# The last image's softmax done one row of sub-images at a time, in another order of sub-images, with spills and one x load issued later

## The chip, the cores and the metric

The kernel runs on one core of a Trainium2 chip. The metric is device time in microseconds (us) of one execution, and lower is better. TensorE is called PE, VectorE DVE, ScalarE ACT, GpSimd POOL and SyncE SP. Line numbers such as L1211 are those of the kernel before, unless the text says that they are those of the changed one.

## The reference

Two layers follow each other on x, of 4 images, 256 channels and 64 by 64 pixels, all in 32 bits.

```python
# layer 0: 49 logits per pixel, then attention over a dilated 7x7 window
k = conv(x, w1, padding=6, rhs_dilation=2) + b1       # 256 -> 128, 7x7
k = conv(k, w2) + b2                                  # 128 -> 49, 1x1
attn = softmax(k, axis=1)
xp = pad(x, 6)
shifts = stack([xp[:, :, 2*u:2*u+64, 2*v:2*v+64] for u in range(7) for v in range(7)], axis=1)
x = einsum('bkchw,bkhw->bchw', shifts, attn)
# layer 1: iterative whitening in 4 groups of 64 channels
Sigma = EPS * I + cov(x - mean);  rTr = 1 / trace(Sigma)
P = I;  5 times: P = 1.5 P - 0.5 P^3 (Sigma rTr)
out = (P sqrt(rTr)) (x - mean) * weight + bias
```

## The kernel before

**Convolution.** The two convolutions of layer 0 are one 7 by 7 convolution from 256 channels to 49 logits. It is done by evaluation at points: DVE (L347 to L354) and ACT (L541, L547) evaluate x at the points (`xh`), PE multiplies each bank of points by its weights `wr` (L599, into the two PSUM tiles `cv`), ACT and DVE take the banks out (`pv`, L610), and DVE interpolates (`zz`, `lgx`). ACT adds the bias at L731, after which an image's logits are complete. Each image has rows of banks, three banks to a row.

**Sub-images.** Since the window is dilated by 2, an image splits into four sub-images of 32 by 32 pixels by the parity of row and column. Sub-image n = 4b, ..., 4b + 3 of image b is (h, pc): h is the parity of the row and picks one of two x slots of the image, pc is the parity of the column. The order is (0, 0), (0, 1), (1, 0), (1, 1).

**Softmax.** `softmax(b, pc)` turns the logits of one column parity, both rows h, to pixels on partitions (PE, L991), and does maximum, Exp, sum and scaling. For images 0 to 2 ACT does the Exp in 16 pieces with the bias taken in; for the last image DVE subtracts the maximum (L1006) and ACT does Exp over each row at once (L1013). Four DVE shuffles (L1035) follow over both rows together; the result is `d`.

**Terms and bands.** `move_terms(n)` copies the terms of one sub-image into `zt` in eleven copies, on ACT for images 0 to 2 (L1076) and on DVE for the last (L1088). Eight POOL DMAs write them to DRAM (`sd`, L1093; two buffers that alternate over n). `load_band(n, half)` reads them back with SP DMAs as the banded matrices `band` (L1128) and `bandz` (L1139). There is one buffer for each half.

**Weighted sum.** `make_block` turns a block of x by PE (L1169) and evicts it into `xb` (L1175) and, for the middle blocks, `xbz` (L1183); `xb` has four buffers, and the turned tiles `tp` in PSUM have three. These evictions are ACT's for images 0 to 2 until the convolution is over, and from then on (`tail`) DVE's. `weighted_sum` multiplies blocks by bands (L1211) into `y`. `store_y` puts y back into the x slot (ACT L1231; in the tail its second half on DVE, L1229). `turn_y` turns it (PE L1242) and ACT copies it into `yt` (L1250), and `moments` accumulates the covariance `sig` (PE L1263).

**Halves.** Each sub-image is done by `first_half(n)` and `second_half(n)`, written here as f0, s0, f1, s1 and so on. A first half also turns the last four tiles of the sub-image before and adds their moments; `finish()` does the same where no first half follows. In a first half the order on PE is: turn 4 and 5 of the sub-image before, matmuls of block (0,0), block (1,0), turn 6, matmuls of (0,1), block (1,1), turn 7, block (2,0), matmuls of (1,0), block (2,1), matmuls of (1,1), matmuls with `bandz`, store, moments, blocks (3,0) and (3,1). A second half ends by turning the first two blocks of the next sub-image.

**Order.** PE runs its instructions in the order in which the program is written. On the other engines a scheduler orders them by priority, and each engine's queue is then run in that order. The convolution of image b is cut into eight stretches, and `gap(b, j)` after each runs what `plan` put there: the softmax of image b - 1 in gaps 0 and 1, and halves of the sub-images before. For image 2 its halves are planned from gap 4 of image 3 on, so f8 is in gap 4, s9 in gap 7, and f10 follows the convolution. After the convolution comes the tail: f10, the softmax for pc 0 of the last image, s10, the softmax for pc 1, f11, s11, f12 and so on to s15, all in the order of `todo`. Then layer 1's iterations run (some 664 to 677 us), and the result is made and stored (677 to 728 us).

**x slots.** Images use slots of x in SBUF. After an image's row is stored, `move(k)` for k = 0, 1, 2 spills the slot's y to DRAM (POOL, L1281, 2 MB in one DMA) and loads the x of slot 5, 6 or 7 into its place from a DRAM copy, `ahead` (POOL, L161). `load_x` loads x from the input in four POOL DMAs (L147). The spilled slots come back in the tail. POOL issues its DMAs in the order of its queue, and the profile shows 0.53 us for each `sd` write and 1.69 us for each `load_x` piece.

Of the kernel before, what the change touches and what calls it, by code (L numbers as in the profile page):

```python
# [32 lines left out]
def kernel(  # L33
# [29 lines left out]
    nc = tc.nc  # L63
# [875 lines left out]
        "p (q r c w) -> p q r c w", q=Q8, r=2, c=NCC  # L939
    )  # L940
    row_eval(0, 5, [rb[0], rb[1], xrs[5]])
    for s in range(2):
        load_x(s, s, nc.gpsimd)
    col_interp(0, 1)
    col_interp(0, 2)
    direct0(4, 1)
# [30 lines left out]
        yt_buf.append(a)  # L977


    def softmax(b, pc):  # L980

        lv = logits[b].rearrange("p r w -> p (r w)")
        nm = f"{b}_{pc}"
        mx = work.tile([P, NCH, 2], F32, tag="mx", name=f"mx_{nm}")
        lt = []
        for hf in range(2):
            t = cv_buf[hf] if b == B - 1 else tp()
            lt.append(t.rearrange("p (i h k) -> p i h k", i=NI, h=2))
            for i in range(NI):
                pe(  # L990
                    nc.tensor.transpose(  # L991
                        lt[hf][:, i].rearrange("p h k -> p (h k)")[:, :K2],
                        lv[:K2, bass.ds(2 * (NI * hf + i) * P + pc, P, 2)],
                        ident[:K2, :K2],
                    )
                )
            nc.vector.tensor_reduce(
                mx[:, NI * hf : NI * (hf + 1)], lt[hf][:, :, :, :KT], AX.X, ALU.max
            )
        nc.vector.tensor_scalar(mx, mx, -1.0, None, ALU.mult)  # L1000
        d = terms[b, pc] = bpool.tile([P, 2, NCH, KT], F32, tag="d", name=f"d_{nm}", bufs=2)
        s = work.tile([P, 2, NCH], F32, tag="s", name=f"s_{nm}")
        if b == B - 1:
            for hf in range(2):
                half = slice(NI * hf, NI * (hf + 1))
                nc.vector.tensor_tensor(  # L1006
                    d.rearrange("p h i k -> p i h k")[:, half],
                    lt[hf][:, :, :, :KT],
                    mx[:, half].unsqueeze(3).to_broadcast([P, NI, 2, KT]),
                    ALU.add,  # L1010
                )
            for h in range(2):
                nc.scalar.activation(d[:, h], d[:, h], AF.Exp)  # L1013
                nc.vector.tensor_reduce(s[:, h], d[:, h], AX.X, ALU.add)
        for h in range(2):
            for i in range(NCH) if b < B - 1 else ():
                nc.scalar.activation(  # L1017
                    d[:, h, i], lt[i // NI][:, i % NI, h, :KT], AF.Exp,
                    bias=mx[:, i, h : h + 1], accum_out=s[:, h, i : i + 1],
                )  # L1020
            nc.vector.reciprocal(s[:, h], s[:, h])
            rm = work.tile([P, NCH, KS], F32, tag="rm", name=f"rm_{nm}_{h}")
            nc.vector.tensor_tensor(
                rm,
                s[:, h].unsqueeze(2).to_broadcast([P, NCH, KS]),
                cmask.unsqueeze(1).to_broadcast([P, NCH, KS]),
                ALU.mult,
            )
            dh = d[:, h].rearrange("p i (u v) -> p i u v", u=KS)
            nc.vector.tensor_tensor(  # L1030
                dh, dh, rm.unsqueeze(2).to_broadcast([P, NCH, KS, KS]), ALU.mult
            )
        dv = d.rearrange("p h i (u v) -> p (h i u) v", u=KS)
        for step, vs in ((1, slice(4, 7, 2)), (2, slice(5, 7)), (-1, slice(0, 3, 2)), (-2, slice(0, 2))):
            last = nc.vector.stream_shuffle(  # L1035
                dv[:, :, vs], dv[:, :, vs], [(c - step) % SW for c in range(SW)]
            )

        return last

    terms, moved, loaded = {}, set(), set()

    MOVES = [(0, 0, 4), (2, 0, 2), (2, 2, 2)]
    MOVES += [(s, j, 1) for s in (1, 3) for j in range(CR)]

    def move_terms(n, after=None):

        b, h, pc = n // 4, n // 2 % 2, n % 2
        if n in moved or n >= 4 * B or (b, pc) not in soft_done:
            return  # L1050
        moved.add(n)
        zt = zts[n % 2]
# [3 lines left out]
        for k, (s, j0, nj) in enumerate(MOVES):  # L1056
            u = (s + R) % CR
            m, g = divmod(j0 + u - R, CR)
            ne = 2 if u + CR < KS else 1
            i = d[j0 * SW : (j0 + nj) * SW, :, u : u + CR * (ne - 1) + 1 : CR]  # L1060
            i = bass.AP(
                tensor=i.tensor,
                offset=i[:, :, :, KS - 1].offset,
                ap=[*(list(a) for a in i.ap[:-1]), [-1, KS]],
            )
            o = zt[g * SW : (g + nj) * SW]
            e = R + KS * m + KS - 1 - u
            o = bass.AP(
                tensor=o.tensor,
                offset=o[:, e].offset,  # L1070
                ap=[list(o.ap[0]), [KS * WS, NCH], [(KS - CR) * WS, ne], [1, KS]],
            )

            with tc.high_priority() if n == 0 else nullcontext():
                if b < B - 1:
                    ins = nc.scalar.copy(o, i)  # L1076
                    if after is not None:

                        tc.add_manual_dep(
                            ins.ins,  # L1080
                            after.ins.name,
                            mybir.DependencyInfo(
                                mybir.DependencyClass.NoSync, mybir.DependencyReason.DATA
                            ),
                            reason="move_terms",
                        )
                else:
                    nc.vector.tensor_copy(o, i)  # L1088
        D = sd[n % 2][:]
        for g in range(CR):  # L1090
            for h in range(2):
                p0 = g * SW + h * TC
                nc.gpsimd.dma_start(  # L1093
                    bass.AP(
                        tensor=D.tensor,
                        offset=D.offset + h * HS + g * RS,
# [3 lines left out]
                        "p (m e) w -> p m (e w)", e=KS  # L1100
                    ),
                )

    back = []

# [11 lines left out]
    def load_band(n, half):  # L1117
# [28 lines left out]
            )  # L1146
        if (n, half) == (4 * B - 1, 1):
            bring_back(dma)

    blocks = {}  # L1150

    tail = []

    def tile_of(t, cc, t8, h, pc):

# [1 line left out]

    def where(n):

        return slots[n // 2], n % 2  # L1160

    def make_block(n, m):

# [3 lines left out]
        for cc in range(NCC):  # L1167
# [2 lines left out]
                    t[:, cc * P : (cc + 1) * P], tile_of(xt, cc, t8, h, pc), ident  # L1170
                )
            )
        xb = bpool.tile([P, C], F32, tag="xb", name=f"xb_{n}_{t8}{h}", bufs=4)
        with tc.high_priority():
            (nc.vector.tensor_copy if tail else nc.scalar.copy)(xb, t[:, :C])  # L1175
        blocks[n, m] = xb
        if t8 in (1, 2):
            z = ("z", 2 - t8)
# [1 line left out]
                blocks[n, z] = bpool.tile([P, C], F32, tag=f"xbz{t8}", name=f"xbz_{n}_{t8}")  # L1180
            i = slice(0, 64) if t8 == 2 else slice(64, P)
            with tc.high_priority():
                (nc.vector.tensor_copy if tail else nc.scalar.copy)(  # L1183
                    blocks[n, z][h * 64 : (h + 1) * 64], t[i, :C]
                )

# [89 lines left out]
    def move(k):  # L1276

        nxt_k = {0: 5, 1: 6, 2: 7}.get(k)
        if nxt_k is not None:
            spill[k] = dram.tile([P, NCC * SH * W], F32, name=f"spill{k}")  # L1280
            nc.gpsimd.dma_start(spill[k], slots[k].rearrange("p a r w -> p (a r w)"))  # L1281
            load_x(k, nxt_k, nc.gpsimd)

    open_n, done, soft_done = [], {-1}, set()

    half_done = {-1}

# [6 lines left out]
        if n % 2:  # L1294
            move(n // 2)

    def first_half(n):
        last = open_n.pop() if open_n else None

        def turn(i):  # L1300
            if last is not None:
                turn_y(last, i)

        for m in PIECES[0][:2]:
            if (n, m) not in blocks:
                make_block(n, m)
        turn(4)
        turn(5)
        weighted_sum(n, 0, 0)
        make_block(n, PIECES[0][2])  # L1310
        turn(6)
        weighted_sum(n, 0, 1)
        make_block(n, PIECES[0][3])
        turn(7)
        make_block(n, PIECES[1][1])
        weighted_sum(n, 0, 2)
        make_block(n, PIECES[1][2])
        weighted_sum(n, 0, 3)
        weighted_sum(n, 0, 4)
        move_terms(n + 1, store_y(n, 0))  # L1320
        half_done.add(n)
        load_band(n + 1, 0)
        if last is not None:
            moments(last, 1)
            if last % 2:
                move(last // 2)
        make_block(n, PIECES[1][3])
        make_block(n, PIECES[1][4])

    def bands(n, after=None):  # L1330

# [4 lines left out]
            load_band(n, 1)  # L1336
            move_terms(n + 1, after)

    def second_half(n):
        turn_y(n, 0)  # L1340
        turned = turn_y(n, 1)
        if n % 4 == 3:
# [5 lines left out]
        turn_y(n, 3)  # L1348
        weighted_sum(n, 1, 3)
        weighted_sum(n, 1, 4)  # L1350
        last = store_y(n, 1)
        moments(n, 0)
        open_n.append(n)
# [5 lines left out]


    NPC = 8
    todo = {}

    def plan(b, j, *what):
        todo.setdefault((b + j // NPC, j % NPC), []).extend(what)

    def soft(b, pc):
        with tc.high_priority() if pc == 0 else nullcontext():
            last = softmax(b, pc)
        soft_done.add((b, pc))  # L1370
        if pc == 0 and (b == 0 or tail):
            bands(4 * b)

    for b in range(B):
        hs = [
            (lambda n=n, f=f: f(n))
            for n in range(4 * b, 4 * b + 4)
            for f in (first_half, second_half)
        ]
# [5 lines left out]
                    plan(b + 1, 2 + j, finish)  # L1385
        else:
            for j in range(8):
                plan(b + 1, 4 + j, hs[j])
    for b in range(B):
        for j in range(2) if b else ():  # L1390
            plan(b + 1, j, lambda b=b, j=j: soft(b, j))
    plan(1, 2, lambda: load_x(4, 4, nc.gpsimd))
# [39 lines left out]
        slots[k] = rpool.tile([P, NCC, SH, W], F32, name=f"back{k}")  # L1432
        back.append(k)
    tail.append(True)
    for k in sorted(todo):
        gap(*k)
    finish()


# [215 lines left out]
```

## Time and profile before

| | |
|---|---|
| median of three runs | 741.35 us (739.52 to 743.1) |
| the profiled execution | 735.81 us, of which the span is 734.0 us |
| PE / DVE / ACT / POOL busy | 684.0 / 598.0 / 328.8 / 133.2 us |
| mean granted clock of PE | 0.977 |
| last convolution matmuls (L599) end | 554.1 us |
| logits of the last image complete (L731) | 565.2 us |
| first halves f10, f11, f12, f13 | 9.65, 20.08, 9.04, 7.88 us |
| second halves s9 to s13 | 6.0 to 6.3 us |

The span runs from the first to the last instruction of the profiled execution. Shares of busy time are over that span. The granted clock is a share of PE's full speed. In a line of the timeline the first number is the start and the second the duration of a group of instructions, and the brackets name the idle time of that engine just before and what ended it.

### The profile page before, as it was taken

Reading aid. Unit: us, or ns where it says so; the run is one execution under the profiler, and the core shown is the slowest. Engines: PE = TensorE matmul, PEld = TensorE weight load, DVE = VectorE, ACT = ScalarE, POOL = GpSimd, SP = SyncE. Lnnn points to the kernel's source line nnn. Section 1 sums busy time; section 2 is a strip of 40 time slices with the busy share of each in tenths; the row PEclk is TensorE's granted clock in tenths of the full one; section 3 lists DMA queues with packets and bytes.
Section 4 is the critical chain, followed back from the end, with each engine's and each line's share of the span. In section 5 each row is a group of like instructions: output and inputs, shape, how many; then the busy total and the mean of one; then the engine's idle time right before and its main releaser. Section 6 shows DMA issues by size and latency. Waiting matters only on the chain.

```text
span 734.0 us, 19103 instructions
## 1 busy us (share of the span) xinstructions
PE 684.0 (93%) x7728; PEld 539.1 (73%) x7728; DVE 598.0 (81%) x1291; ACT 328.8 (45%) x919; POOL 133.2 (18%) x194
## 2 busy tenths in 40 slices
PE   6999999999898999998999999998999689997996
PEld 1449543478898988897999989888998678885231
DVE  3799998995796899999886899899998885435575
ACT  1424320133654655675545445716546222332564
POOL 0002526663021020020220200200211322100000
PEclk9999999999999999999999999999999979997899
DMA  8923999973665582157645820452641535472687
GB/s 322 259 92 103 239 387 212 229 179 90 169 173 150 206 299 68 60 188 257 173 111 201 266 69 1 104 168 72 166 103 37 106 75 126 107 271 117 246 354 316
DMA packets 78337, 126.10 MB, mean 172 GB/s; under 512 B 36471, under 2 KB 58664, under 8 KB 77096
## 3 DMA queue, kind: packets, MB, share of 16 engines
q1 hardware_dynamic: 59912, 64.52, 26.9%
q0 software_dynamic: 12288, 42.08, 21.8%
q10 hardware_dynamic: 6048, 18.27, 8.0%
q8 instruction: 61, 1.00, 0.5%
q14 instruction: 28, 0.23, 0.1%
HBM read 78.78 MB, written 52.36 MB: 179 GB/s over the span
## 4 chain that ended last, share of the span: by engine, by line
PE 38%; DVE 27%; issue 9%; ACT 6%; DMA 4%; POOL 4%; ACTq 0%; SPq 0%; POOLq 0%; DVEq 0%
PE cv L599 15%; PE y L1211 7%; PE tp L1595 4%; DVE xh L354 3%; PE tp L1242 3%; DMA band<-sd 3%; DVE pv L354 3%; POOL ahead L147 3%; PE sig L1263 3%; DVE zz L354 2%; PE tp L1169 2%; DVE rb L347 2%; DVE rb L354 2%; ACT d L1017 1%; DVE pv L350 1%
## 5 line engine op out<-in xcount | busy, mean ns | idle before, releaser
L599 PE MATMUL cv<-xh,wr 128*49 128x128 f32 x4160 | 231.5, 273 | 3.5 <-ACT xh L547 3.3
L599 PEld LDWEIGHTS cv<-xh,wr 128*49 128x49 f32 x4160 | 226.3, 124 | 6.9 <-ACT xh L547 3.5
L1211 PE MATMUL y<-band,xb 128*128 128x209 f32 x512 | 113.4, 348 | 7.0 <-DMA band<-sd 5.9
L1093 POOL DMA_DIRECT2D sd<-zt x128 | 67.3, 532 | 234.1 <-ACT zt L1076 159.9
L1211 PEld LDWEIGHTS y<-band,xb 128*128 128x128 f32 x512 | 87.8, 195 | 8.9 <-DMA band<-sd 4.8
L610 ACT COPY pv<-cv 113x486 f32<-113x486 f32 (+2 forms) x60 | 26.1, 435 | 95.6 <-PE cv L599 90.5
L1250 ACT COPY yt<-tp 128x256 f32<-128x256 f32 x128 | 45.4, 378 | 50.3 <-PE tp L1242 49.2
L1242 PE MATMUL tp<-ident,slot 128*128 128x128 f32 x256 | 51.4, 298 | 9.0 <-ACT yt L1250 6.7
L354 DVE SCALAR_TENSOR_TENSOR pv<-pv 113x162 f32<-113x162 f32 x176 | 53.1, 322 | 3.3 <-ACT pv L610 2.6
L1242 PEld LDWEIGHTS tp<-ident,slot 128*128 128x128 f32 x256 | 41.1, 205 | 15.9 <-ACT yt L1250 7.8
L1169 PE MATMUL tp<-ident,slot 128*128 128x128 f32 x256 | 50.0, 300 | 2.7 <-DVE xbz L1183 1.4
L1231 ACT ACTIVATE slot<-y,pivot 128x512 f32<-128x512 f32 x52 | 36.1, 741 | 34.5 <-PE y L1211 34.4
L1169 PEld LDWEIGHTS tp<-ident,slot 128*128 128x128 f32 x256 | 40.9, 204 | 6.2 <-DVE xbz L1183 1.8
L147 POOL DMA_DIRECT2D slot<-in_x_dram x20 | 33.9, 1695 | 50.6 <-issue 46.2
L1076 ACT COPY zt<-d 32x112 f32<-32x112 f32 (+2 forms) x132 | 38.2, 290 | 7.3 <-DVE d L1035 5.4
L1263 PE MATMUL sig<-yt 128*64 128x65 f32 x1024 | 37.7, 228 | 0.0
L1263 PEld LDWEIGHTS sig<-yt 128*64 128x64 f32 x1024 | 33.2, 140 | 5.7 <-issue 4.3
L354 DVE SCALAR_TENSOR_TENSOR xh<-ct 128x512 f32<-128x512 f32 x40 | 26.7, 689 | 12.4 <-PE cv L599 12.3
L1017 ACT ACTIVATE d<-tp,mx 128x49 f32<-128x49 f32 x96 | 27.5, 337 | 19.8 <-DVE mx L1000 19.8
L764 PE MATMUL acc<-slot,tap 128*49 128x256 f32 (+7 forms) x224 | 34.8, 468 | 0.0
L1175 ACT COPY xb<-tp 128x256 f32<-128x256 f32 x82 | 28.5, 376 | 11.6 <-PE tp L1169 11.1
L1229 DVE TENSOR_SCALAR slot<-y,pivot 128x512 f32<-128x512 f32 x12 | 9.0, 751 | 27.2 <-ACT slot L1231 27.1
(239 smaller groups left out, 1117.3 us busy)
## 6 DMA issues: line engine op xcount, KB each, us to landing
out_dram<-out SPq DMA_DIRECT2D x32, 512.0 KB, 3.6
band<-sd SPq DMA_DIRECT2D x64, 242.0 KB, 3.3
slot<-in_x_dram POOLq DMA_DIRECT2D x20, 512.0 KB, 7.1
sd<-zt POOLq DMA_DIRECT2D x128, 77.0 KB, 3.1
wr<-gd ACTq DMA_DIRECT2D x14, 588.0 KB, 5.3
wr<-gd ACTq DMA_DIRECT2D x14, 490.0 KB, 4.3
ahead<-in_x_dram POOLq DMA_DIRECT2D x12, 512.0 KB, 7.3
spill<-slot POOLq DMA_DIRECT2D x3, 2048.0 KB, 7.2
```

Of the source, the lines that this page charges most:

```text
L147: queue.dma_start(o[:, cc, h], src[:, :, pr, h * SW : (h + 1) * SW])
L354: return in_turn(STT(o, a, f, b, ALU.mult, ALU.add))
L599: nc.tensor.matmul(o, wv[:, sc, sr, cc], xv[bc][:, h * NCC + cc], start=(j == 0), stop=(j == len(terms) - 1), skip_group_check=True,)
L1017: nc.scalar.activation(d[:, h, i], lt[i // NI][:, i % NI, h, :KT], AF.Exp, bias=mx[:, i, h : h + 1], accum_out=s[:, h, i : i + 1],)
L1076: ins = nc.scalar.copy(o, i)
L1093: nc.gpsimd.dma_start(bass.AP(tensor=D.tensor, offset=D.offset + h * HS + g * RS, ap=[[LS, TC], [CR * RS, NCH], [1, KS * WS]],), zt[p0 : p ...
L1169: nc.tensor.transpose(t[:, cc * P : (cc + 1) * P], tile_of(xt, cc, t8, h, pc), ident)
L1211: nc.tensor.matmul(ps[:, cc, q0 : q0 + nq, c0:c1], xb[:, cc * P : (cc + 1) * P], rhs, start=(k == 0), stop=(k == len(PIECES[half]) - 1), s ...
L1231: last = nc.scalar.activation(o, i, AF.Identity, bias=pivot[:, cc : cc + 1])
L1242: nc.tensor.transpose(t[:, cc * P : (cc + 1) * P], tile_of(yt, cc, i // 2, i % 2, pc), ident,)
L1250: return nc.scalar.copy(yb.rearrange("p a g c -> p (a g) c")[:, :, :GW], t[:, :C].rearrange("p (e c) -> p e c", c=GW),)
L1263: nc.tensor.matmul(sig[g * GW : (g + 1) * GW, cc], yb[:, cc, g, :GW], yb[:, cc, g], start=(count[0] == 0 and cc == 0), stop=(count[0] == 4 ...
```

## The change

- **Order of the last image.** `place(n)` gives the sub-images of the last image in the order (0, 0), (1, 0), (0, 1), (1, 1), so that both rows of column parity 0 come first. Sub-image 12 is as before; 13 and 14 change places.
- **Softmax by rows.** For the last image `softmax_rows` works on one row h of a column parity: two half reductions, two half subtractions on DVE, one Exp on ACT, sum, scaling, and four shuffles of half the size. Its parts run at chosen places. Row 0 of pc 0 is within s10, ahead of its store; row 1 of pc 0 is issued after the zt copies of sub-image 12; row 0 of pc 1 is at the end of f12, and row 1 after s12.
- **Plan.** The halves of image 2 are planned one gap earlier: f8 in gap 3, s9 in gap 6, f10 in gap 7, and s10 is the first half in the tail.
- **Blocks ahead.** After s11, `finish()` and then all eight blocks of sub-image 12 are turned, into tiles of the pool that later holds the output, before f12.
- **Evictions.** In the tail, xb of sub-images 12 to 15 is on DVE and xbz of them on ACT; of sub-image 11 xbz is on DVE and xb on ACT; both of sub-image 10 are on ACT.
- **Writes.** Of sub-image 12's eight `sd` writes four go to SP's queue.
- **Spills.** `move(k)` orders its spill behind the last `sd` write that POOL was given before it. In POOL's queue spill 0 and its reload now follow the writes of sub-image 3, spill 1 those of 5 and spill 2 those of 7; the reload of slot 1 comes behind the first write of 6, and that of slot 2 behind spill 2.
- **One x load.** The load of slot 1 (image 0, row parity 1) is issued after the last band load of sub-image 0, between the POOL writes of sub-images 0 and 1, where before it stood near 145 to 153 us.

The diff, cut to its core:

```diff
-    for s in range(2):
-        load_x(s, s, nc.gpsimd)
+    load_x(0, 0, nc.gpsimd)
...
+    def softmax_rows(b, pc, lt, h):
+        nm = f"{b}_{pc}"
+        d = terms[b, pc][:, h]
...
+        for t, o in zip(lt, half):
+            nc.vector.tensor_reduce(mx[:, o], t[:, :, h, :KT], AX.X, ALU.max)
+        for t, o in zip(lt, half):
+            nc.vector.tensor_tensor(
+                d[:, o],
+                t[:, :, h, :KT],
+                mx[:, o].unsqueeze(2).to_broadcast([P, NI, KT]),
+                ALU.subtract,
+            )
+        nc.scalar.activation(d, d, AF.Exp)
+        nc.vector.tensor_reduce(s, d, AX.X, ALU.add)
+        scale_terms(nm, h, d, s)
+        shuffle(d.rearrange("p i (u v) -> p (i u) v", u=KS))
+        soft_done.add((b, pc, h))
...
+    def place(n):
+
+        b, k = divmod(n, 4)
+        return (b, k % 2, k // 2) if b == B - 1 else (b, k // 2, k % 2)
...
-                nc.gpsimd.dma_start(
+                queue = nc.sync if h and n == 4 * (B - 1) else nc.gpsimd
+                dma = queue.dma_start(
...
+                if queue is nc.gpsimd:
+                    written[:] = [dma]
...
+        if (n, half) == (0, 1):
+            behind(load_x(1, 1, nc.gpsimd), dma.ins.name)
...
-        xb = bpool.tile([P, C], F32, tag="xb", name=f"xb_{n}_{t8}{h}", bufs=4)
+        if n == 4 * (B - 1):
+            k = 2 * t8 + h
+            if k % 4 == 0:
+                ahead_xb.append(
+                    rpool.tile([P, 4, C], F32, tag="out", name=f"xbs_{k}", bufs=6)
+                )
+            xb = ahead_xb[-1][:, k % 4]
+        else:
+            xb = bpool.tile([P, C], F32, tag="xb", name=f"xb_{n}_{t8}{h}", bufs=4)
         with tc.high_priority():
-            (nc.vector.tensor_copy if tail else nc.scalar.copy)(xb, t[:, :C])
+            (nc.vector.tensor_copy if n >= 4 * (B - 1) else nc.scalar.copy)(xb, t[:, :C])
...
-                (nc.vector.tensor_copy if tail else nc.scalar.copy)(
+                on_dve = tail and n < 4 * (B - 1)
+                (nc.vector.tensor_copy if on_dve else nc.scalar.copy)(
...
-            nc.gpsimd.dma_start(spill[k], slots[k].rearrange("p a r w -> p (a r w)"))
+            dma = nc.gpsimd.dma_start(spill[k], slots[k].rearrange("p a r w -> p (a r w)"))
+            tc.add_manual_dep(
+                dma.ins,
+                written[0].ins.name,
+                mybir.DependencyInfo(mybir.DependencyClass.NoSync, mybir.DependencyReason.DATA),
+                reason="move",
+            )
...
             for j in range(8):
-                plan(b + 1, 4 + j, hs[j])
-    for b in range(B):
+                if b == B - 1 or 3 + j >= NPC:
+                    rest.append(hs[j])
+                else:
+                    plan(b + 1, 3 + j, hs[j])
+    for b in range(B - 1):
...
-    for k in sorted(todo):
-        gap(*k)
...
+    n = 4 * last_b
+    rest[0](lambda: soft_start(0, True))
+    with tc.high_priority():
+        move_terms(n)
+    with tc.issue_after(moved_by[n].ins):
+        soft_rows(1, 0)
+    rest[1]()
+    move_terms(n + 1)
+    rest[2]()
+    finish()
+    for t8 in range(4):
+        for h in range(2):
+            if (n, (t8, h)) not in blocks:
+                make_block(n, (t8, h))
+    rest[3](lambda: soft_start(1, False))
+    rest[4]()
+    soft_rows(1, 1)
+    for f in rest[5:]:
+        f()
     finish()
```

`soft_start(pc, first)` turns the logits of pc (`turned_logits`, eight PE transposes into the two `cv` tiles) and runs `soft_rows(0, pc)`. The halves take it as an argument and run it after their last matmuls, ahead of `store_y`.

## The prediction

> **What bounds the kernel now.** The shares of the span come first, then PE's waits, then the order of time around the long ones.
>
> ```profile
> PE 684.0 (93%) x7728; PEld 539.1 (73%) x7728; DVE 598.0 (81%) x1291; ACT 328.8 (45%) x919; POOL 133.2 (18%) x194
> ```
>
> PE is the bound, so the change is worth the PE waits that it takes away, less those that it makes. PE's waits by releaser (total us, count, longest):
>
> ```profile
> PE tp L1242 <- ACT yt L1250: 6.7, 2, 5.9
> PE y L1211 <- DMA band<-sd: 5.9, 4, 2.0
> PE cv L599 <- ACT xh L547: 3.3, 1, 3.3
> PE y L1211 <- DVE xbz L1183: 2.1, 6, 0.4
> ```
>
> The longest lies in the first half of sub-image 11 (f11; "s" is a second half). The timeline there (start, us, engine, line, tiles; the idle time before it in brackets), PE's first, then ACT's and DVE's:
>
> ```profile
> 580.16 0.39 PE L1169 MATMUL tp<-ident,slot 128*128 128x128 f32 x2
> 586.45 0.70 PE L1242 MATMUL tp<-ident,slot 128*128 128x128 f32 x2 [5.91 <-ACT yt L1250]
> 588.58 0.70 PE L1169 MATMUL tp<-ident,slot 128*128 128x128 f32 x2 [1.42 <-DVE xbz L1183]
> ```
> ```profile
> 585.19 0.95 ACT L1013 ACTIVATE d<-d 128x392 f32<-128x392 f32 x2 [6.27 <-DVE d L1006]
> ```
> ```profile
> 580.80 2.48 DVE L1088 COPY zt<-d 128x56 f32<-128x56 f32 x11
> 584.12 1.04 DVE L1006 TENSOR_TENSOR d<-cv,mx 128x392 f32<-128x392 f32 x2
> ```
>
> Read backwards: PE waits for a yt copy, ACT has the Exp of the softmax for pc 1 ahead of it, and that Exp waits for a subtraction that DVE reaches only after its shuffles and the eleven zt copies of sub-image 12. The windows show what the wait does to the clock (span, busy us of PE, PEld, DVE, ACT, POOL, granted clock, DMA share, GB/s):
>
> ```profile
> 580.00:586.00 6.00, 0.55 (x4) 0.35 (x2) 5.13 (x18) 0.81 (x2) 2.81 (x6) 0.85 0.23 32
> 586.00:590.00 4.00, 2.12 (x7) 1.71 (x8) 3.94 (x14) 0.77 (x3) 1.38 (x3) 0.50 0.49 110
> 341.00:344.00 3.00, 3.00 (x16) 2.84 (x15) 3.00 (x8) 1.64 (x5) 0.57 (x1) 0.64 0.38 70
> ```
>
> The third window follows f4's two band waits, and the last fence has the 3.3 us wait within the convolution:
>
> ```profile
> 337.00 0.98 PE L1211 MATMUL y<-band,xb 128*128 128x209 f32 x4 [1.28 <-DMA band<-sd]
> 340.49 0.98 PE L1211 MATMUL y<-band,xb 128*128 128x209 f32 x4 [2.05 <-DMA band<-sd]
> ```
> ```profile
> 497.44 5.45 PE L599 MATMUL cv<-xh,wr 128*49 128x128 f32 x96 [3.27 <-ACT xh L547]
> ```
>
> An undisturbed first half takes 7.48 us (f13 takes 7.88, of which 0.40 is an xbz wait). Against that f10 took 9.65, f11 20.08 (577.77 to 597.85), f12 9.04, and f13 to f15 0.40 too much each: 2.17, 12.6, 1.56 and 1.2 us. Of f11's 12.6 the waits (5.91, 1.42, 0.83, 0.22) are 8.4 and the half clock behind them 4.2.
>
> **What the change takes away.**
>
> *f11.* Only row h 0 of pc 0 is now due before f11, the other row follows the zt copies, and pc 1 moves to f12's end. In the changed kernel's instruction order DVE has, from logits turned at V to the last xbz of f11: two half reductions 0.6, a store 0.75, two half subtractions 0.6, the sum 0.55, reciprocal, rm and product 0.95, four xbz 1.6 and three half shuffles 1.1, with some 1.5 of waiting for Exp, which stands behind two yt copies: V+7.7. PE starts f11 at V+1.75 and wants that xbz 5.0 us in (where f8's z matmuls came due), at V+6.75. About 1.0 us of wait stays, too short for the clock to fall: gain 11.6.
>
> *f12.* Its blocks are turned ahead. Its terms: after the xbz, a shuffle 0.36, eleven zt copies 2.48 and the store of f11 that stands between them 0.72, so ready at V+11.25, 9.5 us after f11 starts. Four writes on POOL beside four on SP end 2.1 us on (4 x 0.53), land 3.1 on (page), and the band follows, 1.0 to issue and 3.3 to land: 19.0 us after f11's start. PE is there after f11 8.5, s11 6.2, 0.6 for the store that the four turns wait for, 2.7 for those turns and their sig, and 2.3 for six blocks: 20.3. The slack is 1.3, less than the 1.4 by which the band's landing at 602.3 (4.67) passed the median, so I charge 0.5 (bounds 0 and 7: 3 late, with f11's 4.2 of clock). Of f12's 1.56 the store's 0.6 stays: gain 1.0. With eight writes on POOL the band would be 2.1 us later and the slack gone.
>
> *f10, f13 to f15.* xbz of the last image goes to ACT, beside xb on DVE: the three 0.40 go, 1.2. Of f10's 2.17 its ACT copies keep about 1.0, as the 0.87 of f8's z matmuls does: gain 1.2.
>
> *The wait at 494.* f8 comes one bank earlier, at PE's 492, and 8 us of its work stand where xh was late: gain 3.3, bounds 0 and 3.3, since DVE is busy 8.97 of the 9 us before. The last banks then end 2.8 us later (554.14 + 6.09 of s9 - 3.27 = 556.96) and so may the logits (565.15 before, so 568). They are wanted after f10 and most of s10, 569.5 to 571.6: no wait by that, 0.5 charged (0 to 3).
>
> *f4.* The 2 MB spill of slot 1 went out at 322.35, just ahead of sub-image 4's writes:
>
> ```profile
> spill<-slot POOLq DMA_DIRECT2D x1, 2048.0 KB, 6.9
> sd<-zt POOLq DMA_DIRECT2D x8, 77.0 KB, 6.0
> ```
>
> (issues from 320 to 345 us, last number the median landing). The writes took 6.0 against the page's 3.1, and the eighth waited 1.28 more. With the spill behind sub-image 5's writes both go, 4.2 us, more than the two waits (3.33) and the clock behind them (3 us at 0.64, 1.1). The whole would be 4.4; DVE is busy 7.00 of 7.00 us from 334 to 341 and takes part of it back, so I take half, 2.2. The spill then runs beside band 5, issued at 357 to 363 and wanted at 372: hidden. The reloads come later, but their first readers (ACT at 280, 410 and 427) are later too in the new order, or 9 us behind; with slot 1's first load, now four issues of 1.69 us between sub-images 0 and 1, I charge 0.5 (0 to 6.8, and below nothing to -1.7, f0's own band wait beside x loads).
>
> Taken away: 11.6 + 1.0 + 1.2 + 1.2 + 3.3 + 2.2 = 20.5 us.
>
> **What it adds.** The pc 1 softmax does not vanish. From pc 1's logits, turned at U at the end of f12, DVE's order has ahead of xb (1,1) of sub-image 13: four half reductions and four half subtractions 2.4, two sums 1.1, reciprocals and rm 0.8, two products 1.1, eight half shuffles 2.85, 22 zt copies 5.0, two stores 1.45 and three xb 1.2: 16 us in one queue. PE wants that block after s12 (6.2) and 4.1 us into f13 (in f8 the same matmuls came at 506.94, from 502.82), at U+10.3. So PE loses 5.7 us there, some 1.7 on the stores and first xb, and 4.0 at a stretch on xb (1,1). The clock may follow. The 3.27 wait at 494 left it at 1.00, the 5.91 halved it for 4.2 us of loss, f4's 1.28 and 2.05 cost 1.1: 4.0 lies nearest the first but above it, and I take 2.0 (0 to 4.2). Together 7.7. The Trainium skill, "TensorE: Matmul & The Clock Gate", Part 1, has the clock halved after an idle window of about 3.4 us and released after a busy one of that length; as an estimate that is 1.7 us here and a sum 0.3 lower. The 3.27 and 5.91 agree with it; f4's fall to 0.64 after no wait over 2.05 does not, and there the measurement decides.
>
> Added: 7.7 + 0.5 + 0.5 + 0.5 = 9.2. The profiled execution was 735.81 us (span 734.0 and 1.8 around it): 735.8 - 20.5 + 9.2 = 724.5. It lies 5.5 us under the median of the three runs, 741.35; by that median 730.
>
> **Rivals.**
>
> *The DVE batch blocks PE twice (slower).* One mechanism: an Exp in ACT's queue and a batch on DVE ahead of PE's evictions. If f11 is not cured, since Exp still stands ahead of yt copies, and f13 becomes a second f11 with the whole 12.6, the sum is 735.8 - 20.5 + 11.6 + 12.6 + 1.5 = 741.0, by the median 746.5. It decides once new waits pass 20.5 + 3.7 = 24.2 us. For it: 16 us of DVE against 10.3 of PE. Against it: xbz, stores and xb stand between the pieces, and Exp waits for one row.
>
> *f13 is cheap.* xb rides between the pieces and PE loses 3 us without the clock: 735.8 - 20.5 + 3 + 1.5 = 719.8, by the median 725.3. Against it: xb (1,1) stands behind the last copy.
>
> *DVE keeps the early gains.* DVE is full from 334 to 341 and from 485 to 500; if it sets the logits' time, the 3.3 and 2.2 come back as a wait in s10: 730.0, by the median 735.5.
>
> *Band 12 is late* by 3 us and halves the clock: 724.5 + 6.5 = 731, by the median 736.5. For it: a slack of 1.3 on a chain of 19.
>
> **How the numbers follow.** Forecast 0.50 (722 to 735), f13 cheap 0.14, DVE keeps the gains 0.12, band late 0.10, blocked twice 0.14. A measurement of this kernel tells some 0.5% from no change, 3.7 us, so faster is under 737.6 and slower over 745.1. The forecast, the cheap f13, nearly 0.09 of the third and 0.05 of the fourth are faster, 0.78; the rest of those two is the same, 0.08; slower is 0.14. The range of 720 to 740 leaves out the slow case and about 0.05 of ends.
>
> **What would show it.** Right: no wait of PE on yt in f11 over 1.5 us; f4 without band waits and at clock 1.00; no wait on xh near 494; band 12 waiting under 1 us; in f13 some 4 us before the matmuls with xb (1,1), released by a DVE xb copy. Wrong: PE waiting for a logits row in s10, an f11 above 10 us, an f13 above 18 or under 9, a wait on a reloaded slot, or a stage after the last sig (664 to 734 before) of another length.

## The result and the profile after

The changed kernel takes 737.73 us in the median (734.92 to 740.37), the kernel before in the same runs 740.28: a ratio of 0.9961, 95% interval 0.9943 to 0.9979. It is faster by 0.4%, 2.9 us at that ratio, where 11.3 us were forecast. The profiled execution of the changed kernel took 738.35 us, span 736.3, near its median; that of the kernel before, 735.81, lay 3.1 us under the fastest of its thirteen timed runs. So the stages are compared in the two profiles, and the whole by the timed runs.

PE's waits in the changed kernel, by releaser (total us, count, longest). L1298 is `turn_y` there, L1267 the weighted sum, L1230 and L1239 the evictions xb and xbz, L1306 yt, L1285 the half of `store_y` on DVE, L998 the logits' turn:

```profile
PE y L1267 <- ACT xbz L1239: 7.1, 11, 1.5
PE tp L998 <- ACT xb L1230: 4.3, 2, 2.2
PE y L1267 <- DVE xb L1230: 4.1, 1, 4.1
PE tp L1298 <- ACT yt L1306: 3.9, 3, 2.9
PE tp L1298 <- DVE slot L1285: 3.6, 5, 1.3
PE y L1267 <- DMA band<-sd: 3.4, 2, 2.0
```

The 5.9 on yt in f11 and the 3.3 on xh are gone from the list, and the band waits fell from 5.9 to 3.4. In their place stand a 4.1, a 2.9 and five waits for a store, and the two waits on xb at the logits' turn grew from 2.0 to 4.3 together. Where they lie (PE's timeline):

```profile
343.64 0.98 PE L1267 MATMUL y<-band,xb 128*128 128x209 f32 x4 [1.37 <-DMA band<-sd]
...
499.51 0.51 PE L1298 MATMUL tp<-ident,slot 128*128 128x128 f32 x2 [2.93 <-ACT yt L1306]
...
587.21 0.69 PE L1267 MATMUL y<-bandz,xbz 128*128 128x96 f32 x4 [1.46 <-DVE xbz L1239]
...
598.20 1.75 PE L1298 MATMUL tp<-ident,slot 128*128 128x128 f32 x7 [1.34 <-DVE slot L1285]
...
625.93 1.76 PE L1267 MATMUL y<-band,xb 128*128 128x209 f32 x4 [4.14 <-DVE xb L1230]
```

They are f4, f8, f11, the `finish()` after s11, and f13. The same stretches, each from its first matmul to the first of the next, in us:

| | before | changed | three edits (below) |
|---|---|---|---|
| f4 | 12.60 | 9.30 | |
| f8, with the xh wait before | 11.5 | 12.1 | 8.2 |
| f10 | 9.65 | 9.15 | |
| s10 with pc 0's logits | 6.94 | 7.48 | |
| f11 | 20.08 | 8.87 | |
| s11 | 6.16 | 7.09 | |
| finish, blocks, f12, pc 1's logits | 9.99 | 12.26 | |
| s12 | 6.29 | 6.86 | |
| f13 | 7.88 | 15.24 | |
| f10 to f13 | 67.0 | 67.0 | 59.2 |

f11 lost 11.2 us as forecast, and the halves around it took all of it back: f13 7.4, the stretch from the finish to f12 2.3, s10 to s12 2.0 together, less 0.5 of f10.

Ahead of f10 the changed kernel lost as well: f10 starts at 563.99, in the profile of before at 560.23. Of these 3.8 us 1.4 are clock in f1 (last section), 0.4 lie between the matmuls ahead of f3 and the end of f4, 0.9 at the logits' turn at 471 (a wait of 2.18 on xb for 1.29), 0.6 in f8 and 0.5 in f9.

What holds f13 is in DVE's queue, eleven zt copies of sub-image 15 ahead of xb:

```profile
622.75 2.67 DVE L1128 COPY zt<-d 128x56 f32<-128x56 f32 x11
625.45 1.09 DVE L1230 COPY xb<-tp 128x256 f32<-128x256 f32 x3
```

What holds f8 is in ACT's queue, an xh copy that waits for DVE ahead of f8's yt copies:

```profile
498.19 0.66 ACT L541 COPY xh<-rb 128x512 f32<-128x512 f32 x1 [6.98 <-DVE rb L354]
...
499.08 0.65 ACT L1306 COPY yt<-tp 128x256 f32<-128x256 f32 x2
```

### The profile page after: what moved, and what is told of

It reads as the page before. It is cut to its first block, busy times and chain, and to the rows that moved or that the text cites. A ratio compares the mean times of both kernels' runs of the same rounds, so it can differ in the third digit from the quotient of the medians.

```text
span 736.3 us, 19131 instructions
## 1 busy us (share of the span) xinstructions
PE 686.7 (93%) x7728; PEld 542.4 (74%) x7728; DVE 588.3 (80%) x1278; ACT 341.4 (46%) x954; POOL 131.4 (18%) x190
## 5 line engine op out<-in xcount | busy, mean ns | idle before, releaser
L1135 POOL DMA_DIRECT2D sd<-zt x124 | 65.5, 534 | 345.8 <-ACT zt L1116 279.1
L1267 PE MATMUL y<-band,xb 128*128 128x209 f32 x480 | 105.4, 346 | 7.8 <-DVE xb L1230 4.1
L1267 PEld LDWEIGHTS y<-band,xb 128*128 128x128 f32 x480 | 81.7, 194 | 9.1 <-DVE xb L1230 4.3
L1306 ACT COPY yt<-tp 128x256 f32<-128x256 f32 x128 | 45.3, 379 | 40.4 <-PE tp L1298 39.1
L1298 PE MATMUL tp<-ident,slot 128*128 128x128 f32 x256 | 52.3, 301 | 8.7 <-ACT yt L1306 3.9
L1298 PEld LDWEIGHTS tp<-ident,slot 128*128 128x128 f32 x256 | 41.2, 204 | 16.6 <-ACT yt L1306 5.2
L1230 ACT COPY xb<-tp 128x256 f32<-128x256 f32 x96 | 33.5, 375 | 13.8 <-PE tp L1216 13.0
L1319 PE MATMUL sig<-yt 128*64 128x65 f32 x1024 | 39.5, 233 | 0.0
L1319 PEld LDWEIGHTS sig<-yt 128*64 128x64 f32 x1024 | 34.8, 146 | 5.8 <-issue 4.4
L764 PE MATMUL acc<-slot,tap 128*49 128x256 f32 (+7 forms) x224 | 34.7, 468 | 0.0
L764 PEld LDWEIGHTS acc<-slot,tap 128*49 128x49 f32 x224 | 16.2, 123 | 17.9 <-issue 15.5
```

The costliest lines, as they stand in the source:

```text
L764: nc.tensor.matmul(ps[h * HB : h * HB + KT, :, o0:o1], w[v][:, cc], rhs, start=(j == 0 and k == 0), stop=(j == len(order) - 1), skip_group ...
L1135: dma = queue.dma_start(bass.AP(tensor=D.tensor, offset=D.offset + h * HS + g * RS, ap=[[LS, TC], [CR * RS, NCH], [1, KS * WS]],), zt[p0 : ...
L1267: nc.tensor.matmul(ps[:, cc, q0 : q0 + nq, c0:c1], xb[:, cc * P : (cc + 1) * P], rhs, start=(k == 0), stop=(k == len(PIECES[half]) - 1), s ...
L1298: nc.tensor.transpose(t[:, cc * P : (cc + 1) * P], tile_of(yt, cc, i // 2, i % 2, pc), ident,)
L1306: return nc.scalar.copy(yb.rearrange("p a g c -> p (a g) c")[:, :, :GW], t[:, :C].rearrange("p (e c) -> p e c", c=GW),)
L1319: nc.tensor.matmul(sig[g * GW : (g + 1) * GW, cc], yb[:, cc, g, :GW], yb[:, cc, g], start=(count[0] == 0 and cc == 0), stop=(count[0] == 4 ...
```

## The experiments

Each ran beside the kernel before; the ratio is to that kernel, so the changed kernel stands at 0.9961 throughout. A and B are the two theories of the expectation. Line numbers in a run's lines are those of that run.

**The shift of the plan undone.**

```diff
-                if b == B - 1 or 3 + j >= NPC:
+                if b == B - 1 or 4 + j >= NPC:
...
-                    plan(b + 1, 3 + j, hs[j])
+                    plan(b + 1, 4 + j, hs[j])
...
+    rest.pop(0)()
     rest[0](lambda: soft_start(0, True))
```

> The changed kernel with the halves of image 2 planned one gap later again (f8 in gap 4 as in the kernel before; f10 is the first half of the tail). Theory A (the shift gains nothing: xh of that bank is late on DVE, and in the changed kernel ACT's queue has the xh copy that waits for it ahead of f8's yt copies, so PE waits inside f8 instead): within 1.5 us of the changed kernel's 737.7, PE waiting 3 us on xh again and f8 back under 9 us. Theory B (the shift gains the 3.3 us of the prediction and the loss is elsewhere): 3.3 us slower, 741.

742.58 us, ratio 1.0027 (1.0011 to 1.0043): 4.9 us slower than the changed kernel, more than B's 3.3, and not for B's reason. PE waited 3.75 for xh and f8 ran through, as A had it; but f11 waited for band 11. SP's timeline of this run shows what the load stood behind:

```profile
588.20 0.34 SPq L1135 DMA_DIRECT2D sd<-zt  x1
588.71 0.37 SPq L1172 DMA_DIRECT2D band<-sd  x1
```
```profile
593.02 1.76 PE L1267 MATMUL y<-band,xb 128*128 128x209 f32 x4 [10.05 <-DMA band<-sd]
```

A write of sub-image 12, put on SP's queue, waits there for zt, and the load of band 11 is behind it. In ACT's queue of the same run the Exp of pc 0's second row waits 7.34 us for DVE in f11, so the band was not the only thing in the way.

**The same with all of sub-image 12's writes on POOL.**

```diff
-                queue = nc.sync if h and n == 4 * (B - 1) else nc.gpsimd
+                queue = nc.gpsimd
```

> The changed kernel without the shift of the plan and with all eight writes of sub-image 12 on POOL. Without the shift alone PE waited 10.05 us in f11 for band 11, because the write of 12 stood at the head of SP's queue, waiting for zt, ahead of that band's load. Theory A (the shift gains nothing by itself, and the 742.6 of the run without it were this SP queue): the 10 us wait goes, 1.5 to 5 us come back as a wait for band 12 in f12, and the time is 735 to 739, no slower than the changed kernel. Theory B (the shift is worth its 3 to 5 us): still 741 or more.

745.65 us, ratio 1.0061 (1.0038 to 1.0083). The band wait went, and another stood in its place. PE's line, then ACT's:

```profile
590.46 0.70 PE L1298 MATMUL tp<-ident,slot 128*128 128x128 f32 x2 [7.22 <-ACT yt L1306]
```
```profile
589.34 0.53 ACT L1067 ACTIVATE d<-d 128x392 f32<-128x392 f32 x1 [7.33 <-DVE d L1061]
```

That is the stall of the kernel before, in the same place of f11: without the shift, the scheduler again put an Exp that waits for DVE ahead of f11's yt copies, here that of pc 0's second row. A's number was wrong. What the shift is worth by itself isn't told by these two runs, since each brought a stall of its own.

**All writes on POOL, with the shift.** The edit of the run before, in the changed kernel.

> The changed kernel with all eight writes of sub-image 12 on POOL. By the prediction the band is 2.1 us later and its slack of 1.3 is gone: 0.8 us slower than the changed kernel, at most 2. Since in the changed kernel f12 began with no wait for the band, and its first matmuls came 9 us after the band loads were issued at 595.5, theory A says that the slack is larger than 2.1: within 1.5 us of 737.7 and no band wait in f12.

737.78 us, 0.9968 (0.9945 to 0.9992): no change that can be told, and no band wait in f12. The second queue was not needed: the first load of band 12 is issued 14.9 us after f11's start in both runs (594.59 here, 595.51 in the changed kernel). The Trainium skill, "DMA: Bandwidth & Descriptors", section "Issuing engines are not separate DMA queues", says that issuing from several engines saves only the sequencer's time, since all run on the same 16 engines; the run agrees, and here even the 2.1 us of issue brought nothing.

**Spills and slot 1's x load as before.**

```diff
+    for s in range(2):
+        load_x(s, s, nc.gpsimd)
-    load_x(0, 0, nc.gpsimd)
...
-        if (n, half) == (0, 1):
-            behind(load_x(1, 1, nc.gpsimd), dma.ins.name)
...
-            tc.add_manual_dep(
-                dma.ins,
-                written[0].ins.name,
-                mybir.DependencyInfo(mybir.DependencyClass.NoSync, mybir.DependencyReason.DATA),
-                reason="move",
-            )
```

> The changed kernel with spills issued as early as before and slot 1's x loaded early again. Theory A (the reordering takes f4's band waits and the clock behind them away, and this reaches the end): 2 to 4 us slower than the changed kernel, 740 to 742, with f4 at 12 us or more. Theory B (DVE is full in that stretch and takes it back, or the later spill and load cost as much elsewhere): within 1.5 us of 737.7 although f4 is longer.

737.02 us, 0.9971 (0.9952 to 0.9989): B. The late spill shortens f4 and lengthens what stands before it. First this run, then the changed kernel, whose clock is 0.82 from 324 to 328 and 0.88 from 328 to 336 (1.00 in both in the kernel before):

```profile
322.83 0.73 PE L999 MATMUL tp<-ident,lgx 113*128 113x113 f32 x4 [0.69 <-ACT xb L1229]
323.49 11.56 PE L599 MATMUL cv<-xh,wr 128*49 128x128 f32 x208
338.99 1.76 PE L1266 MATMUL y<-band,xb 128*128 128x209 f32 x4 [3.26 <-DMA band<-sd]
```
```profile
326.89 1.03 PE L998 MATMUL tp<-ident,lgx 113*128 113x113 f32 x4 [2.08 <-ACT xb L1230]
327.85 12.57 PE L599 MATMUL cv<-xh,wr 128*49 128x128 f32 x208
```

Ahead of that xb copy the changed kernel's ACT queue has zt copies that wait for DVE's shuffle; in this run the same copies, at 319.52, don't wait:

```profile
323.60 1.17 ACT L1116 COPY zt<-d 128x56 f32<-128x56 f32 x4 [1.40 <-DVE d L986]
```

From the convolution at 305.67 in this run (308.34 in the changed kernel) to its restart after f4 (348.70, 349.65) the changed kernel gains 1.7 us; in the first half before (f3) it had lost 1.0 (from the matmuls of L764, at 283.85 and 285.52, to that convolution: 21.8 and 22.8). Another 0.9 goes at the logits' turn near 471, where the wait on xb is 1.31 here and 2.18 in the changed kernel. So the gain is 1.7 and the loss 1.9.

**One xh copy on DVE.** Point 0 of bank 0, in the last image's fourth row.

```diff
+        cur["late"] = (b, br) == (B - 1, 3)
...
-            nc.scalar.copy(o[0], X4[0])
+            (nc.vector.tensor_copy if cur.get("late") else nc.scalar.copy)(o[0], X4[0])
```

> The changed kernel with one copy moved: xh of point 0 of bank 0 in the fourth row of the last image, which waits in ACT's queue for DVE ahead of f8's yt copies, is done by DVE itself (0.4 to 0.7 us there). Theory A (that copy is why f8 takes 12.1 us in place of 7.5): the 2.9 us wait on yt and the half clock behind it go, f8 under 9 us, and the banks behind it find xh ready: 2.5 to 4.5 us faster than the changed kernel, 733 to 735. Theory B (DVE's xh is late all the same): PE waits as long on xh behind f8, within 1.5 us of 737.7.

734.48 us, 0.9922 (0.9894 to 0.995): A. f8 takes 8.25 us (495.01 to 503.26), its only wait of note is

```profile
500.89 0.69 PE L1268 MATMUL y<-bandz,xbz 128*128 128x96 f32 x4 [0.88 <-ACT xbz L1240]
```

the first yt copies come 3.5 us earlier on ACT, ahead of the xh copy that DVE now makes,

```profile
495.56 0.65 ACT L1307 COPY yt<-tp 128x256 f32<-128x256 f32 x2
```
```profile
500.99 0.42 DVE L541 COPY xh<-rb 128x512 f32<-128x512 f32 x1
```

and PE finds xh ready behind f8. That xh was late on DVE at 494 was hidden by f8 once f8's own copies no longer queued behind it.

**The second row of pc 1 later.**

```diff
-    soft_rows(1, 1)
-    for f in rest[5:]:
+    rest[5]()
+    with tc.issue_after(evicted[n + 1, (2, 1)].ins):
+        soft_rows(1, 1)
+    for f in rest[6:]:
```

> The changed kernel with the second row of pc 1's softmax issued behind the eviction of block (2,1) of sub-image 13, in place of after s12; with it the eleven zt copies of sub-image 15 leave the queue ahead of xb (1,1) of 13. Theory A (f13's 7.8 us too much are DVE's queue and the clock behind the wait): f13 under 9.5 us, no half clock in it, 4 to 7 us faster than the changed kernel, 731 to 734. Theory B (that work only blocks another half later): f13 short but f14 longer by as much, within 1.5 us of 737.7.

733.61 us, 0.9912 (0.989 to 0.9935): 3.6 us less than the changed kernel by the ratios, 4.1 by the medians. A holds in kind: f13 fell from 15.24 to 11.1 us (611.8 to 622.87) and f14 did not grow for it (8.7, of which 0.82 is a wait for the store). It is not as short as expected, since the first row of pc 1 and its zt copies still stand ahead of f13's first store (a wait of 1.62), and the clock from 612 to 620 is 0.79.

**Stores of sub-images 10 to 12 on ACT.**

```diff
-                if tail and cc:
+                if tail and cc and n > 4 * (B - 1):
```

> The changed kernel with both halves of store_y of sub-images 10, 11 and 12 on ACT (before: one of them on DVE behind the softmax rows). Theory A (the turns of s11, the lone finish, s12 and f13 wait 0.8, 1.3, 0.5 and 0.8 us for that store, and the clock falls to half after the second): those waits go, each replaced by at most 0.7 us for the second ACT store, and the stretch from s11 to f12 is 3 us shorter: 2 to 4 us faster than the changed kernel, 734 to 736. Theory B (the waits only move to ACT): within 1.5 us of 737.7.

733.62 us, 0.9916 (0.9893 to 0.9939): A. The four waits for a store are gone but for 0.20, PE's clock from 596 to 604 is 1.00 in place of 0.79, and from f10 to f13 it takes 61.9 us in place of 67.0. Part of that is f13 (13.4 for 15.2), where the waits are now 1.52 and 2.76.

**Both of these edits.**

> The late second row of pc 1 and store_y of sub-images 10 to 12 on ACT, together. Alone each took 4 us off the changed kernel. Theory A (two separate places, f13 and s11 to f12): the gains add, 728.5 to 731. Theory B (the stores on ACT already shorten DVE's batch ahead of f13, so both remove part of the same wait): 731 to 733.

729.91 us, 0.9863 (0.9834 to 0.9892): the gains add.

**No blocks turned ahead.**

```diff
-        if n == 4 * (B - 1):
+        if False:
...
-    for t8 in range(4):
-        for h in range(2):
-            if (n, (t8, h)) not in blocks:
-                make_block(n, (t8, h))
```

> The changed kernel without the blocks turned ahead: f12 turns its own blocks (two before it, six inside), in the four xb buffers, after the lone finish. Theory A (turning ahead only moves the same six blocks in front of f12; the band is there in any case, since the run with all writes on POOL showed no wait for it): the first matmul of f12 comes 2 us earlier and waits at most 2 us for band 12, and the time is within 1.5 us of the changed kernel's 737.7. Theory B (the blocks are the cover of band 12): 2 to 4 us of band wait in f12, 739.5 to 742.

730.81 us, 0.9882 (0.9857 to 0.9907): neither, 5.8 us faster by the ratios. Band 12 is in time, as A had it, and finish to f12 takes as long as in the changed kernel. The gain is in f13, which the edit leaves alone: 9.6 us (615.53 to 625.11). DVE's order came out otherwise there, with shuffles and copies behind xb in place of ahead:

```profile
620.50 0.75 DVE L1230 COPY xb<-tp 128x256 f32<-128x256 f32 x2
...
623.17 2.30 DVE L1128 COPY zt<-d 128x56 f32<-128x56 f32 x10
```

**Both rows of pc 0 at once.**

```diff
             soft_rows(0, pc)
+            if first:
+                soft_rows(1, pc)
...
-    with tc.issue_after(moved_by[n].ins):
-        soft_rows(1, 0)
```

> The changed kernel with both rows of pc 0's softmax done together in s10, ahead of the zt copies of sub-image 12 (no split in time of the two rows). Theory A (the row split is what keeps f11 at 8.9 us): both Exp stand ahead of f11's later yt copies and DVE's two rows, 8 us, ahead of its xbz evictions, so f11 waits 3 to 5 us, band 12 is 4 us later, and the time is 3 to 8 us above the changed kernel, 741 to 746. Theory B (the order of sub-images and the move of pc 1 out of f11 do it): within 1.5 us of 737.7.

735.19 us, 0.992 (0.9896 to 0.9944): A is refuted, and B's number is missed too, by the ratios 3.0 us below the changed kernel. f11 takes 9.15 us for 8.87, with 1.16 and 0.26 of waits for xbz; band 12 makes f12 wait 1.50. f13 is 3.9 us shorter (616.16 to 627.53), again by an order of DVE with xb between the pieces. The split of the rows in time is not what cured f11. In both orders the Exp ahead of f11's later yt copies finds its subtraction done, where in the kernel before it waited 6.27 us for one behind the zt copies:

```profile
582.50 0.95 ACT L1067 ACTIVATE d<-d 128x392 f32<-128x392 f32 x2
```

**Three edits together**: the late row, the stores on ACT, the xh copy on DVE.

> Three edits together: the late second row of pc 1, store_y of sub-images 10 to 12 on ACT, and the one xh copy on DVE. Alone they took 4.1, 4.1 and 3.2 us off the changed kernel, the first two together 7.8. Theory A (three separate places): 10.5 to 11.5 us off, 726 to 728. Theory B (an earlier convolution only brings the end of it up against DVE, so that the tail starts no sooner): 729 to 730 as without the xh copy.

727.29 us, 0.9826 (0.9801 to 0.985), the lowest median of all: A. The last convolution matmuls end at 559.7 and sub-image 13's first half 59.2 us later. In the windows from 596 to 604 and from 620 to 628, where the changed kernel had 0.79 and 0.72 of the clock, it is at 1.00:

```profile
596.00:604.00 8.00, 7.36 (x55) 6.71 (x53) 3.40 (x10) 2.78 (x6) 0.14 (x1) 1.00 0.30 71
620.00:628.00 8.00, 7.19 (x71) 6.55 (x70) 6.48 (x26) 2.51 (x6) 2.45 (x5) 1.00 0.47 120
```

(span, busy us of PE, PEld, DVE, ACT, POOL, clock, DMA share, GB/s). It is not at 1.00 throughout: behind f11's wait of 1.67 for xbz it has 0.84 from 580 to 588, where the changed kernel had 1.00.

**The three, with the old spills.**

> The three edits together, with spills and slot 1's x load as early as in the kernel before. Theory A (the later spills bring nothing on balance, as the run with old spills alone said): within 1.5 us of the kernel with the three edits, 726 to 728.5, with f4 3 us longer and the wait for xb in the softmax for image 1's second column parity 1.4 us shorter. Theory B (they were hidden only by what waited later): 2 to 4 us above it.

727.89 us, 0.9831 (0.9809 to 0.9854): A again, the spills' new place is worth nothing that can be told.

## Why the prediction was wrong

The sign was right and the size was not. Of the 11.3 us the tail from f10 to f13 was to give 5.5; in these profiles it gave none. f4, the xh wait, f14 and f15 were to give the rest, and the stages ahead of f10 lost 3.8.

- **f11** held: 11.2 for 11.6. That the two rows are split is not the reason, though; the run with both rows together shows the same f11. Without the shift of the plan the stall was back at 7.22, so the cure hangs on where the scheduler puts the second Exp. No run moves pc 1's softmax alone, so its share stays open.
- **f13** held: 5.7 and 2.0 of clock were charged, 7.8 over an undisturbed half was measured, with the 4.14 wait on xb (1,1) behind the eleven copies where the 4.0 was placed. The granted clock behind it:

```profile
624.00:632.00 8.00, 6.03 (x51) 5.50 (x52) 3.90 (x13) 2.21 (x6) 4.22 (x8) 0.60 0.65 131
```

The runs add that this cost hangs on an order that edits elsewhere reshuffle: f13 took 9.6 and 11.4 us in two runs that left it alone.
- **f8 and the late xh** failed at the step "8 us of its work stand where xh was late: gain 3.3". Only f8's PE work was weighed. Its yt copies are ACT's, and ACT's queue had the very xh copy that waits for DVE ahead of them. Measured +0.6 in place of -3.3; with that one copy moved, f8 takes 8.25 us and the gain appears. The last banks, placed at 556.96, ended at 564.06.
- **Stores behind the softmax rows** were the missing term. DVE's half of the stores was in the list of f11 and f12, priced at one 0.6 before the finish. Measured were waits of 0.83, 1.34 (shown above) and 0.51; a fourth, of 0.76, is in f13, where 1.7 were charged for the stores and the first xb. The clock behind the second is 0.79:

```profile
590.60 0.63 PE L1298 MATMUL tp<-ident,slot 128*128 128x128 f32 x3 [0.83 <-DVE slot L1285]
609.73 0.63 PE L1298 MATMUL tp<-ident,slot 128*128 128x128 f32 x3 [0.51 <-DVE slot L1285]
616.74 0.83 PE L1298 MATMUL tp<-ident,slot 128*128 128x128 f32 x3 [0.76 <-DVE slot L1285]
```
```profile
596.00:604.00 8.00, 6.42 (x56) 5.16 (x54) 5.33 (x20) 2.30 (x7) 3.91 (x8) 0.79 0.74 178
```

The stretch from finish to f12 was 2.3 longer in place of 0.5 shorter, s11 and s12 together 1.5 longer. The stores on ACT gave 3.3 us by the ratios, part of it in f13.
- **f4**: the stage itself gave 3.3 where 2.2 were charged; the two band waits became one of 1.37, and in f4 the clock stayed up. But the stretches ahead took 3.7 longer than in the kernel before: 1.0 in f3, and 2.7 around the 2.08 wait on xb, of which 1.4 are the longer wait and most of the rest the clock behind it. The wait at 471 cost 0.9 more. The run with the old spills was no slower than the changed kernel. The step that failed is "The spill then runs beside band 5, issued at 357 to 363 and wanted at 372: hidden": PE did not wait for that band, but the new order on ACT and DVE was not looked at.
- **f10** gave 0.5 for 1.2, with a wait of 1.40 for xbz.
- **Band 12**: no wait. Its loads were issued 14.9 us after f11's start, near the 14.7 of the chain (9.5 + 2.1 + 3.1), but PE wanted the band after 24.0 in place of 20.3, held up above all by the store waits and the clock behind them. So the slack was wider than 1.3 for a reason that the prediction did not have.

The stage after the last sig took 68.5 us in place of 69.7. Over all profiles of this case it lies between 68.4 and 70.1, so this says nothing of the change.

The base was off as well: the profiled execution of before was lucky, and 5.5 us to the median were carried over unchanged; the changed kernel's profile shows none of that distance. Which stage gives the 2.9 us of the timed runs, the pair of profiles can't show; that stays open. The runs name places for the 8.4 that are missing: 2.9 to 3.2 at f8 and 3.3 to 4.1 at the stores, f13's part included (by ratios and by medians), and the 2.2 forecast at the spills.

## What to carry to other kernels

A half that fills PE's idle time brings its evictions with it: before counting its PE work as cover, look at what heads the queue of the engine that evicts, and who that waits for. A DMA write put on a second queue must not stand ahead of the loads that PE waits for. And where a scheduler fixes the order of an engine, one edit's measured gain may be another stage's reshuffled order; read the stage, not only the total, and pin the few instructions that matter behind the ones that release PE.

## What the runs showed of the hardware

The same waits can halve the clock in one execution and not in another. In f1 both kernels wait 1.1 and 0.8 us at the same place; the windows from 222 to 236 us, before and changed:

```profile
222.00:236.00 14.00, 12.14 (x152) 10.94 (x150) 10.02 (x18) 7.91 (x20) 1.30 (x3) 1.00 0.60 175
```
```profile
222.00:236.00 14.00, 12.13 (x126) 10.70 (x123) 10.22 (x18) 7.94 (x20) 1.78 (x4) 0.88 0.64 181
```

The second lost 1.4 us by it: f1's moments took 2.00 us in place of 1.15. From the convolution ahead of f1 to its restart behind it twelve of the fourteen profiles of this case take 16.8 to 16.9 us, the changed kernel and the run with the stores on ACT 18.3. At the finish two waits of 1.34 and 0.83, 7 us apart, halved the clock in the changed kernel (moments 2.00), and the same waits in the run with the xh copy moved did not (1.16). The Trainium skill, "TensorE: Matmul & The Clock Gate", Part 1, has a free-running window of about 3.4 us, so that the turn is run-variable; the traces agree with that, while its idle window of that length is not needed: neither wait there is over 1.4 us. One profile and another can thus differ by some 2 us of clock alone (an estimate: 1.4 in f1 and 0.85 at the finish).
